# A graph layer and a relational attention layer on one core: the order of work in the last two turns

## The chip, the cores and the metric

The kernel runs on one core of a Trainium2 chip. The metric is the device time of one execution in microseconds; lower is better. Every time below is in microseconds unless it says otherwise.

## The reference

The input is 64 graphs of 256 nodes with 256 features each (`x`), and an adjacency of 256 x 256 for each graph. Two layers follow each other.

```python
# layer 0: two graph-attention steps, residual, norm, feed-forward of width 1024 (relu), residual, norm
h = _gat(_gat(x, adj, W1, a1), adj, W2, a2)
h = _layernorm(x + h, g_ln1, b_ln1)
x = _layernorm(h + relu(h @ w_ff1 + b_ff1) @ w_ff2 + b_ff2, g_ln2, b_ln2)
# layer 1: attention over 8 heads of 32, values by relation (adj == 0, adj == 1), output projection
attn = softmax(q @ k.T / sqrt(32))
out = sum(((attn * (adj == r)) @ (x @ Wv[r] + bv[r])) for r in range(4))
x = _ln(x + out @ Wo + bo, g1, beta1)
# feed-forward of width 1024 (gelu), residual, norm
return _ln(x + gelu(x @ W1 + b1) @ W2 + b2, g2, beta2)
```

All of it is float32. A short check at the end of the kernel adds up some accumulated sums (`low`, `lowg`, `high`, `other`) into one integer `bad`; if it is above zero, a general and slower version of the program runs (with these inputs it does not).

## The kernel before, in words

Two graphs make a unit, so there are 32 units, 0 to 31. A unit has 512 rows (four blocks of 128; blocks 0 and 1 are the first graph, 2 and 3 the second). The work is a pipeline of turns: turn `y_` runs layer 1 of unit `y_`, the feed-forward of layer 0 of unit `x_ = y_ + 1`, and the graph attention of layer 0 of unit `z = y_ + 2` (`turn`, L1275). In turn 30 there is no `z` any more, and in turn 31 only layer 1 of unit 31 is left, together with pieces of the output feed-forward of unit 30 that turn 30 left over (`left`, `piece`). So the last two turns have less independent work to put side by side than those before.

The order is written out by hand for some engines in each turn: in turns with an `X` for PE, SyncE, VectorE and ScalarE, in turn 31 for PE and SyncE alone. There a scheduler orders VectorE and ScalarE by the order in the program and its own estimates; `behind(name)` (L694) holds the instructions issued inside it until after a marked one. What each engine executes is fixed in the built program: each engine takes its instructions in that order.

Products of two 2 x 2 block matrices are done with seven block products instead of eight, named 1 to 7:

- `hidden_seven` (L908) is the first feed-forward product. Its steps are called `2a 1a 2b 1b 5a 5b 3a 3b 6a 6b 7a 7b 4a 4b`; a and b are the halves of the width. Steps 5, 6, 7 and 4 multiply differences of the features' quarters, which VectorE makes by four subtractions (`sub`, L920, tile `tt`). Each step puts two 128 x 256 products into a bank of PSUM. `taken` (L945) moves them to `h1`: a copy on ScalarE (L950) when it is the first for that quarter of `h1`, an add on VectorE (L947) when it is not. Steps 6, 7 and 4 go on accumulating in the bank of step 1, and 5 and 3 in that of step 2, so each of them needs the bank to have been read. `c`, `d` and `s` are activations of finished quarters (L956).
- `HiddenOut` (L997) is the second. `sums` (L1013) are four sums of quarters of `h1`; the products 1, 2, 5, 6, 3, 7, 4 (L1027) are each added to `y` on VectorE (L1035). Products 1, 6, 7 and 4 share a bank, and 5 and 3 another.
- `Projections` (L1046) does the same for queries and keys (`q1` to `q7`) and values (`v1` to `v7`): sums at L1062, products at L1094, copies at L1081, adds at L1078.

A norm is made of moments on VectorE (L865, L866), two or three small operations on Pool (L876 to L879; L879 adds to `high`), an offset `nm` on VectorE (L884) and the application on ScalarE (L894) or Pool (L891); `affine` multiplies by a row (`times`, L903) and adds one (`plus`, L906). The last norm of units 30 and 31 is done in another way: `finish` (L1245) centres and multiplies (L1249), `finished` (L1253) scales and adds (L1256) and stores each block. To turn rows into features, PE transposes blocks (`turned` L512, `to_features` L528, instructions at L518 and L534), and the result is copied out of PSUM (L535).

The check is written after the last turn (L1783 to L1794).

Of the kernel before, what the change touches and what calls it, by code (L numbers as in the profile page):

```python
# [9 lines left out]
F32 = mybir.dt.float32  # L10
I32 = mybir.dt.int32
AF = mybir.ActivationFunctionType
# [373 lines left out]
def narrow_path(  # L386
# [495 lines left out]
    def offsets(blocks, mv, rs, nm):  # L882
        bt = slice(blocks[0], blocks[0] + len(blocks))
        nc.vector.scalar_tensor_tensor(nm[:, bt], mv[:, bt, 0], -1.0, rs[:, bt], op0=ALU.mult, op1=ALU.mult)  # L884

# [21 lines left out]

    def hidden_seven(u, l, hT, w, bi, func, d, tt):  # L908

# [6 lines left out]
        def moving(n):  # L916
            return tt[:, n * N:(n + 1) * N].rearrange("p (t a r) -> p t a r", t=NB, r=32)

        def sub(n, x_, y_):
            nc.vector.tensor_tensor(moving(n), x_, y_, ALU.subtract)  # L920

        sub(0, quarter[0][1], quarter[0][0])
        sub(1, quarter[1][1], moving(0))
        sub(2, quarter[1][1], quarter[0][1])
        sub(3, quarter[1][0], moving(1))
        halves = range(2)
# [64 lines left out]
        def steps(names):  # L991
            for name in names.split():
                step(name)

# [51 lines left out]
    class Projections:  # L1046
# [28 lines left out]
        def taken(s, x, o, b, ps):  # L1075
            y, ps = s.out(x, o, b), ps.rearrange("p (i n) -> p i n", i=2)
            if (x, o, b) in s.begun:
                mark["projected"] = nc.vector.tensor_tensor(y, ps, y, ALU.add)  # L1078
            else:
                s.begun.add((x, o, b))  # L1080
                nc.scalar.copy(y, ps)  # L1081

# [136 lines left out]
    def out_pieces(u, y, h1):  # L1219

        if u == NG - 2:
            s = [io.tile([P, T, N], F32, tag="y", name=f"sq{u}", bufs=4),
                 work.tile([P, T, WX], F32, tag="wh", name=f"wq{u}")[:, :, :N]]
            s += [io.tile([P, T, N], F32, tag=t, name=f"sq{u}_{t}", bufs=1) for t in ("xq", "aq")]
        else:
            s = out_sums(u, 1)
        end = HiddenOut(u, 1, y, h1, w2s, s)
        end.sums(1, 2, 4, 3)
        for p in (1, 2, 5, 6, 3):
            end(p)  # L1230
            if p == 3:
                n = finish(u, y, 0)
            yield
        end(7)
        finished(u, y, 0, *n)
        yield
        end(4)
        finished(u, y, 1, *finish(u, y, 1))
        yield
# [4 lines left out]

    def finish(u, y, b):  # L1245

        n = norm(u, 3, y, range(b * NB, (b + 1) * NB))
        for t in n[0]:
            nc.vector.scalar_tensor_tensor(y[:, t, :], y[:, t, :], n[1][:, t, 0:1], rg4,  # L1249
                                           op0=ALU.subtract, op1=ALU.mult)  # L1250
        return n

# [22 lines left out]
    def turn(y_, x_, z, rest=None):  # L1275
# [49 lines left out]
        with order:  # L1325
# [17 lines left out]
            if X:  # L1343
                X["hT"], moves = normed_features(x_, 0, X["y"], copied=(1, 3, 5, 7, 9, 11), later=True)
            else:
                scores(0, (0,))
            p("v5")
# [71 lines left out]
            else:  # L1419
                powers(0, (1,))  # L1420
                p("q3 v3")
                powers(0, (2, 3))
                p("q6 v6 q7 v7")
# [51 lines left out]
            out_(1)  # L1475
            piece()
            if Z:
# [6 lines left out]
            if Z:  # L1484
                out(1)
                Z["m"].scores(0)
                Z["m"].scores(1)
                Z["m"].exp(0)
                Z["m"].exp(1)
                out.sums(4)  # L1490
                offsets(*n)
                out(2)
                applied_norm(y, *n, range(T))
                Z["m"].masks(0)
                out(5)
                Z["m"].masks(1)
                Z["m"].shares()
            elif X:
                out.product(5)
                out.sums(3)  # L1500
                out.add(5)
            if X and not Z:
                out(6)
            if not Z:
                applied_norm(y, *n)
            else:
                Z["m"].scaled(WH)
# [7 lines left out]
            elif X:  # L1515
                out.sums(4)
                out(7, 3)
            if not Z:
                piece()
                hT = to_features(y, f"h3T{y_}")  # L1520
                hT = [h.rearrange("p (t a r) -> p t a r", t=T, r=32) for h in hT]
                if not X:
                    affine(y, rg3, rb3)
            if waiting and Z:
# [13 lines left out]
            tt = work.tile([P, HPB, NB * N], F32, tag="e", name=f"tt{y_}_1")  # L1538
            second = hidden_seven(y_, 1, hT, w1s, b1, AF.Gelu, Y, tt.rearrange("p a n -> p (a n)"))
            if X:  # L1540
                out.add(4)
                n = moments(x_, 1, X["y"], range(NB, NB + 1), n)
            h1 = Y["h1"] = work.tile([P, FB, TN], F32, tag="h1", name=f"h1{y_}_1", bufs=1)
            if Z:
                second("2a 1a")
# [11 lines left out]
            else:  # L1557
                if X:
                    n = norm(x_, 1, X["y"], mv=n, rest=range(NB + 1, T))
                second("2a 1a 2b 1b")  # L1560
                second("5a 5b")
                if waiting:
                    affine(waiting[0][1], rg4, rb4)
                    stored(*waiting.pop(), slice(0, T))
                if X:
                    offsets(*n)
                    applied_norm(X["y"], *n, [0])
                second("3a")
                if X:
                    applied_norm(X["y"], *n, [1])  # L1570
                second("3b")
                if X:
                    applied_norm(X["y"], *n, [2, 3], True)
                second("6a 6b ca cb da db 7a 7b")
                if X:
                    X["hT"] = with_ones(to_features(X["y"], f"h2T{x_}", (nc.vector.tensor_copy,) * 2))
# [205 lines left out]

    c = work.tile([P, 4], F32, tag="mv", name="checks")  # L1783
    for n, v in enumerate((low, lowg, high, other)):
        nc.vector.tensor_reduce(c[:, n:n + 1], v, AX.X, ALU.add)
    s = work.tile([P, 1], F32, tag="ve", name="checked")
    nc.vector.tensor_reduce(s, c[:, 0:3], AX.X, ALU.add)
    good = work.tile([P, 2], F32, tag="z", name="good")
    nc.vector.tensor_scalar(good[:, 0:1], s, 1e30, None, op0=ALU.is_le)
    nc.vector.tensor_scalar(good[:, 1:2], c[:, 3:4], 0.25 * NG * T * N, None, op0=ALU.is_le)  # L1790
    nc.vector.tensor_tensor(good[:, 0:1], good[:, 0:1], good[:, 1:2], ALU.mult)
    ps = bank("goodp")
    nc.tensor.matmul(ps[:1, :1], good[:, 0:1], ones[:, 0:1], start=True, stop=True)
    nc.vector.tensor_scalar(bad, ps[:1, :1], -1.0, float(P), op0=ALU.mult, op1=ALU.add)  # L1794


@with_exitstack
# [37 lines left out]
```

## Time and profile before

| what | value |
|---|---|
| runs, device time | 2951.56 median of 3 (2950.34 to 2952.9) |
| the profiled execution, device time | 2950.62 |
| its span in the profile | 2949.0 |
| mean granted clock of TensorE | 0.998 of full |
| TensorE busy | 2921.7, 99% of the span |
| VectorE, ScalarE, Pool busy | 2611.3 (89%), 1897.2 (64%), 625.6 (21%) |
| last product of the output feed-forward ends | 2938.2 |
| last finishing step (L1256) of unit 31 ends | 2942.1 |
| `bad` (L1794) is written | 2943.3 |

In the profile PE is TensorE, DVE VectorE, ACT ScalarE, POOL GpSimd and SP SyncE. A line of a timeline gives start, length, engine, line, operation, the tile written and those read, the shapes, a count of merged instructions, and in brackets the idle time of the engine before it with the instruction that ended it. A wait line gives who waited for whom: total, times, longest. A line of a table by stretches gives the stretch, the sum of busy times, and then for PE, weight loads, DVE, ACT and POOL the busy time and the number of instructions, then the granted clock of TensorE as a share of full speed, the DMA engines' share and GB/s. [...]one step of four passes is 0.86 long.

### The profile page before, as it was taken

How to read it: one execution, taken by the hardware profiler on the slowest of the kernel's cores; microseconds unless marked ns; L12 is line 12 of the kernel's file. 1: busy time of each engine (PE TensorE's matmuls, PEld its weight loads, DVE VectorE, ACT ScalarE, POOL GpSimd, SP SyncE). 2: the span in 40 equal slices, each digit the busy share in tenths (PEclk: the TensorE clock that was granted, in tenths of full speed). 3: DMA queues.
4: the chain of work that ended last, by engine and by line, in shares of the span. 5: the costliest groups of instructions: out<-in, count | busy, mean ns of one | idle time of the engine just before them, and what ended most of it. 6: DMA issues, size and time to landing. Idle time of an engine off the chain costs nothing.

```text
span 2949.0 us, 58651 instructions
## 1 busy us (share of the span) xinstructions
PE 2921.7 (99%) x22206; PEld 2505.9 (85%) x22206; DVE 2611.3 (89%) x5028; ACT 1897.2 (64%) x3983; POOL 625.6 (21%) x931
## 2 busy tenths in 40 slices
PE   9999999999999999999999999999999999999997
PEld 7788888888888888888888888888888888888876
DVE  5889899989899889999898998899998989988887
ACT  5566666676676666666766766766667667667652
POOL 3312221122121122221221211222212212112211
PEclk9999999999999999999999999999999999999999
DMA  5011111111111111111111111111111111111000
GB/s 152 13 30 32 39 32 32 24 40 32 37 30 26 34 34 38 33 31 24 40 32 37 31 28 31 36 36 35 29 23 40 32 37 32 28 30 33 18 8 16
DMA packets 408020, 99.27 MB, mean 34 GB/s; under 512 B 357834, under 2 KB 407220, under 8 KB 407732
## 3 DMA queue, kind: packets, MB, share of 16 engines
q1 hardware_dynamic: 406332, 94.13, 14.8%
q8 instruction: 178, 2.92, 0.4%
q0 software_dynamic: 1056, 1.05, 0.1%
q14 instruction: 110, 0.90, 0.1%
q10 hardware_dynamic: 344, 0.28, 0.0%
HBM read 56.78 MB, written 16.78 MB: 25 GB/s over the span
## 4 chain that ended last, share of the span: by engine, by line
PE 97%; DVE 2%; ACT 1%; DMA 0%; issue 0%; POOL 0%; DVEq 0%; POOLq 0%; ACTq 0%
PE yf L1027 27%; PE h1a L938 15%; PE h1b L938 11%; PE po L1143 8%; PE v L1094 6%; PE qk L1094 6%; PE sp L1115 4%; PE hpp L839 4%; PE ygp L850 4%; PE xpp L772 4%; PE yop L850 4%; PE zo L1146 2%; PE rows L781 1%; DMA first<-in_adj_dram 0%; DVE st L865 0%
## 5 line engine op out<-in xcount | busy, mean ns | idle before, releaser
L1124 ACT ACTIVATE e<-sp 128x512 f32<-128x512 f32 x512 | 271.0, 611 | 71.2 <-issue 43.7
L1128 DVE TENSOR_TENSOR ea<-e,aT 128x1024 f32<-128x1024 f32 x256 | 311.1, 1217 | 1.6 <-ACT e L1124 1.6
L894 ACT ACTIVATE y<-y,nm,rs 128x256 f32<-128x256 f32 x442 | 235.1, 592 | 64.0 <-DVE nm L884 63.2
L947 DVE TENSOR_TENSOR h<-h1a,h 128x512 f32<-128x512 f32 x293 | 197.5, 682 | 81.7 <-PE h1a L938 78.5
L950 ACT COPY h<-h1b 128x512 f32<-128x512 f32 x293 | 175.2, 599 | 124.6 <-PE h1b L938 122.8
L956 ACT ACTIVATE h<-h,cols 128x256 f32<-128x256 f32 x512 | 221.9, 502 | 35.7 <-DVE h L947 31.5
L734 POOL COPY hT<-yt 32x256 f32<-32x256 f32 x244 | 211.3, 866 | 144.8 <-DVE yt L717 132.1
L1081 ACT COPY qk<-qk 128x512 f32<-128x512 f32 x128 | 74.3, 580 | 237.4 <-PE qk L1094 236.6
L865 DVE BATCH_NORM_STATS2 st<-y 128x6 f32<-128x256 f32 x512 | 208.7, 409 | 5.7
L876 POOL TENSOR_SCALAR rs<-mv 128x4 f32<-128x4 f32 (+1 forms) x134 | 41.7, 312 | 805.1 <-DVE mv L866 438.5
L1035 DVE TENSOR_TENSOR y<-yf,y 128x256 f32<-128x256 f32 x448 | 185.9, 415 | 29.8 <-PE yf L1027 29.8
L956 ACT ACTIVATE h<-h1a,cols 128x256 f32<-128x256 f32 x256 | 102.6, 465 | 131.9 <-PE h1a L938 131.9
L1156 POOL TENSOR_TENSOR low<-low,rq 128x16 f32<-128x16 f32 x64 | 13.9, 217 | 811.6 <-DVE rq L1155 811.6
L906 DVE TENSOR_TENSOR y<-y,rb 128x1024 f32<-128x1024 f32 x126 | 163.2, 1295 | 2.2
L1133 DVE TENSOR_TENSOR es<-e 128x1024 f32<-128x1024 f32 x128 | 156.0, 1219 | 0.0
L903 DVE TENSOR_TENSOR y<-y,rg 128x1024 f32<-128x1024 f32 x126 | 153.0, 1214 | 0.0
L877 POOL TENSOR_TENSOR rs<-rs,mhalf 128x4 f32<-128x4 f32 (+1 forms) x134 | 139.5, 1041 | 8.3
L1115 PE MATMUL sp<-qk 32*128 32x256 f32 x2048 | 138.4, 394 | 0.0
L938 PE MATMUL h1a<-tt,wf 128*128 128x256 f32 x512 | 137.7, 392 | 0.0
L1143 PE MATMUL po<-e,v 128*32 128x256 f32 x2048 | 135.5, 382 | 0.0
L1143 PE MATMUL po<-ea,v 128*32 128x256 f32 x2048 | 134.5, 379 | 0.0
L717 DVE STREAM_TRANSPOSE yt<-y 128x256 f32<-128x256 f32 x364 | 128.2, 407 | 0.9 <-ACT y L894 0.7
(288 smaller groups left out, 7738.4 us busy)
## 6 DMA issues: line engine op xcount, KB each, us to landing
hT<-yt SPq DMA_DIRECT2D x666, 32.0 KB, 1.8
y<-in_x_dram SPq DMA_DIRECT2D x32, 512.0 KB, 4.1
xq<-in_x_dram SPq DMA_DIRECT2D x240, 64.0 KB, 2.3
aq<-in_adj_dram SPq DMA_DIRECT2D x240, 64.0 KB, 2.3
out_dram<-y SPq DMA_DIRECT2D x30, 512.0 KB
wf<-in_L_gnn_w_ff_dram SPq DMA_DIRECT2D x2, 1024.0 KB, 7.8
w<-in_L_gnn_W_dram SPq DMA_DIRECT2D x2, 1024.0 KB
first<-in_adj_dram POOLq DMA_DIRECT2D x2, 512.0 KB, 9.0
```

What stands on the lines that cost most here:

```text
L734: nc.gpsimd.tensor_copy(to, at)
L850: nc.tensor.matmul(ps[:, i * F:(i + 1) * F], lhs(t, k), rhs(b, k), start=(k == 0), stop=(k == n - 1))
L865: nc.vector.bn_stats(st[:, t, :], y[:, t, :])
L894: mark["normed"] = nc.scalar.activation(y[:, t, :], y[:, t, :], AF.Identity, bias=nm[:, t:t + 1], scale=rs[:, t:t + 1])
L938: nc.tensor.matmul(ps[:, i * N:(i + 1) * N], w_[:, f * P:(f + 1) * P], m, start=first and i == 0, stop=True, skip_group_check=True)
L956: nc.scalar.activation(y, y if ps is None else ps[:, i * N:(i + 1) * N], func, bias=bi[:, f:f + 1])
L1027: nc.tensor.matmul(s.ps[n][:, i * F2:(i + 1) * F2], a[:, k, i * P:(i + 1) * P], w_[:, k, :], start=n in (1, 2, 5) and i == 0 and k == 0, s ...
L1094: nc.tensor.matmul(ps[:, i * N:(i + 1) * N], l, r, start=n in (1, 2, 5) and i == 0, stop=True, skip_group_check=True)
L1115: nc.tensor.matmul(ps[a][:, j * N:(j + 1) * N], k_[hp, m, j0:j0 + P], q[hp, m, b * N:(b + 1) * N], start=True, stop=True)
L1124: nc.scalar.activation(e[:, a, :], ps[a], AF.Exp, scale=isd)
L1128: nc.vector.tensor_tensor(ea[:, a:a + 2, :], e[:, a:a + 2, :], ab[:, None, :].to_broadcast([P, 2, NB * N]), ALU.mult)
L1143: nc.tensor.matmul(po[hp, m * N:(m + 1) * N], vs[:, hp], w[:, a, j * N:(j + 1) * N], start=(n == 0), stop=(n == len(terms) - 1))
```

## The change

In the last two turns:

- Unit 31's layer-0 feed-forward, in turn 30: sum 4 and product 3 come before sum 3 and product 7.
- Unit 30's hidden layer, in turn 30: the order is now `times` of unit 29's last affine, then steps 3a and 3b, then the offset and the application of unit 31's norm, steps 6a to 7b, and only then `plus` of that affine and the store of unit 29.
- Turn 31, projections: no exponential of the first scores is issued before the copy of v5; the first two stand behind it (mark `placed`, `fifths`), the other two behind the copy of v3. Sums of unit 30's `h1` (1, 2, 4, 3) stand behind the first add of the values (`projected31_v`).
- Turn 31, features of the normed unit: by graph. The transposes of blocks 0 and 1 come before product 4 of unit 30, and steps 2a and 1a of the hidden layer before the transposes of blocks 2 and 3; the copies are of 128 x 256, three on ScalarE and one on VectorE. The four differences are made after that (step name `t`). Before, all eight transposes, two copies of 128 x 512 and the differences came ahead of step 2a.
- Unit 30's `centred` and `finished` of the first graph stand behind unit 31's second offset (`offset`), and the affine of unit 31 behind an add of the hidden layer (`added`).
- Unit 31: `centred` of the first graph comes after product 7's add.
- The check is made in two parts: `low`, `lowg` and `other` are reduced in turn 31 (in the built program beside the second graph's division), `high` after the last centring, and the two comparisons go as both operands into one product of 1 x 1.

The order of the built programs differs nowhere before unit 31's sum 3, which ran at 2835.8 in the profile before; up to there only line numbers differ. The diff, cut to its core:

```diff
-    def hidden_seven(u, l, hT, w, bi, func, d, tt):
+    def hidden_seven(u, l, hT, w, bi, func, d, tt, begin=True):
...
+        if begin:
+            differences()
...
+                if name == "t":
+                    differences()
...
             if (x, o, b) in s.begun:
                 mark["projected"] = nc.vector.tensor_tensor(y, ps, y, ALU.add)
+                mark.setdefault(f"projected{s.u}_{x}", mark["projected"])
             else:
                 s.begun.add((x, o, b))
-                nc.scalar.copy(y, ps)
+                mark["placed"] = nc.scalar.copy(y, ps)
...
-        end.sums(1, 2, 4, 3)
+        if u == NG - 2:
+            with behind(f"projected{NG - 1}_v"):
+                end.sums(1, 2, 4, 3)
+        else:
+            end.sums(1, 2, 4, 3)
         for p in (1, 2, 5, 6, 3):
             end(p)
             if p == 3:
-                n = finish(u, y, 0)
+                n = norm(u, 3, y, range(NB))
             yield
         end(7)
-        finished(u, y, 0, *n)
-        yield
+        if u == NG - 2:
+            yield
+        with behind("out" if u == NG - 1 else "offset"):
+            centred(y, *n)
+            finished(u, y, 0, *n)
+        if u == NG - 1:
+            verdict = checks()
+            yield
         end(4)
-        finished(u, y, 1, *finish(u, y, 1))
+        n = norm(u, 3, y, range(NB, T))
+        centred(y, *n)
+        if u == NG - 1:
+            verdict()
+        finished(u, y, 1, *n)
         yield
...
+    def checks():
+
+        c = work.tile([P, KB * N // 32], F32, tag="rq", name="checks")
+        good = work.tile([P, 2], F32, tag="z", name="good")
+        for n, v in enumerate((low, lowg, other)):
+            nc.vector.tensor_reduce(c[:, n:n + 1], v, AX.X, ALU.add)
+        nc.vector.tensor_add(c[:, 0:1], c[:, 0:1], c[:, 1:2])
+        nc.vector.tensor_scalar(good[:, 1:2], c[:, 2:3], 0.25 * NG * T * N, None, op0=ALU.is_le)
+
+        def verdict():
+            nc.vector.tensor_reduce(c[:, 3:4], high, AX.X, ALU.add)
+            nc.vector.tensor_scalar(good[:, 0:1], c[:, 3:4], c[:, 0:1], 1e30, op0=ALU.add, op1=ALU.is_le)
+            ps = bank("goodp")
+            nc.tensor.matmul(ps[:1, :1], good[:, 0:1], good[:, 1:2], start=True, stop=True)
+            nc.vector.tensor_scalar(bad, ps[:1, :1], -1.0, float(P), op0=ALU.mult, op1=ALU.add)
...
             else:
-                scores(0, (0,))
+                scores(0, ())
             p("v5")
...
-                powers(0, (1,))
+                mark["fifths"] = mark["placed"]
+                with behind("fifths"):
+                    powers(0, (0, 1))
                 p("q3 v3")
-                powers(0, (2, 3))
+                with behind("fifths"):
+                    powers(0, (2, 3))
...
             elif X:
                 out.product(5)
-                out.sums(3)
+                out.sums(4)
                 out.add(5)
...
+            if not X:
+                piece()
+                h3T = work.tile([P, KB, TN], F32, tag="hT", name=f"h3T{y_}")
+                ph = turned(y, f"h3T{y_}", range(NB))
+
+                def half(b_):
+                    ns = slice(b_ * N, (b_ + 1) * N)
+                    nc.scalar.copy(h3T[:, 1, ns], ph[1][:, ns])
+                    (nc.scalar.copy, nc.vector.tensor_copy)[b_](h3T[:, 0, ns], ph[0][:, ns])
+
+                half(0)
...
             elif X:
-                out.sums(4)
-                out(7, 3)
+                out.sums(3)
+                out(3, 7)
...
+            if not X:
+                piece()
             h1 = Y["h1"] = work.tile([P, FB, TN], F32, tag="h1", name=f"h1{y_}_1", bufs=1)
+            if not X:
+                second("2a 1a")
+                turned(y, f"h3T{y_}", range(NB, T), ph)
+                half(1)
+                second("t")
...
-                second("2a 1a 2b 1b")
+                second("2a 1a 2b 1b" if X else "2b 1b")
+                if not X:
+                    with behind("added"):
+                        affine(y, rg3, rb3)
                 second("5a 5b")
                 if waiting:
-                    affine(waiting[0][1], rg4, rb4)
-                    stored(*waiting.pop(), slice(0, T))
+                    times(waiting[0][1], rg4)
+                second("3a 3b")
                 if X:
                     offsets(*n)
                     applied_norm(X["y"], *n, [0])
-                second("3a")
-                if X:
                     applied_norm(X["y"], *n, [1])
-                second("3b")
-                if X:
                     applied_norm(X["y"], *n, [2, 3], True)
                 second("6a 6b ca cb da db 7a 7b")
+                if waiting:
+                    plus(waiting[0][1], rb4)
+                    stored(*waiting.pop(), slice(0, T))
```

More of the change, by code (lines that the diff above doesn't have):

```diff
@@ L883, in offsets @@
         bt = slice(blocks[0], blocks[0] + len(blocks))
-        nc.vector.scalar_tensor_tensor(nm[:, bt], mv[:, bt, 0], -1.0, rs[:, bt], op0=ALU.mult, op1=ALU.mult)
+        mark["offset"] = nc.vector.scalar_tensor_tensor(nm[:, bt], mv[:, bt, 0], -1.0, rs[:, bt], op0=ALU.mult, op1=ALU.mult)
     def applied_norm(y, blocks, mv, rs, nm, part=None, gpsimd=False):
@@ L920, in sub, with differences @@
             nc.vector.tensor_tensor(moving(n), x_, y_, ALU.subtract)
[L922 to L925, printed above, removed]
+        def differences():
+            sub(0, quarter[0][1], quarter[0][0])
+            sub(1, quarter[1][1], moving(0))
+            sub(2, quarter[1][1], quarter[0][1])
+            sub(3, quarter[1][0], moving(1))
+        if begin:
+            differences()
         halves = range(2)
@@ L992, in steps @@
             for name in names.split():
-                step(name)
+                if name == "t":
+                    differences()
+                else:
+                    step(name)
         return steps
@@ L1227, in out_pieces @@
         end = HiddenOut(u, 1, y, h1, w2s, s)
-        end.sums(1, 2, 4, 3)
+        if u == NG - 2:
+            with behind(f"projected{NG - 1}_v"):
+                end.sums(1, 2, 4, 3)
+        else:
+            end.sums(1, 2, 4, 3)
         for p in (1, 2, 5, 6, 3):
@@ L1243, in stored, with centred @@
         nc.sync.dma_start(out[b].rearrange("b (c p) f -> p (b c) f", p=P), y[:, bt, :])
[L1245 to L1249, printed above, removed]
+    def centred(y, blocks, mv, rs, nm):
+        for t in blocks:
+            nc.vector.scalar_tensor_tensor(y[:, t, :], y[:, t, :], mv[:, t, 0:1], rg4,
                                            op0=ALU.subtract, op1=ALU.mult)
-        return n
+    def checks():
[11 more added lines that the diff above has]
+            nc.vector.tensor_scalar(bad, ps[:1, :1], -1.0, float(P), op0=ALU.mult, op1=ALU.add)
+        return verdict
     def finished(u, y, b, blocks, mv, rs, nm):
@@ L1475, in turn @@
             out_(1)
-            piece()
+            if X:
+                piece()
             if Z:
@@ L1503, in turn @@
                 out(6)
+            if not X:
[7 more added lines that the diff above has]
+                half(0)
+                hT = [h3T[:, k].rearrange("p (t a r) -> p t a r", t=T, r=32) for k in range(KB)]
             if not Z:
@@ L1515, in turn @@
             elif X:
-                out.sums(4)
-                out(7, 3)
-            if not Z:
+                out.sums(3)
+                out(3, 7)
+            if X and not Z:
                 piece()
@@ L1521, in turn @@
                 hT = [h.rearrange("p (t a r) -> p t a r", t=T, r=32) for h in hT]
-                if not X:
-                    affine(y, rg3, rb3)
             if waiting and Z:
@@ L1538, in turn @@
             tt = work.tile([P, HPB, NB * N], F32, tag="e", name=f"tt{y_}_1")
-            second = hidden_seven(y_, 1, hT, w1s, b1, AF.Gelu, Y, tt.rearrange("p a n -> p (a n)"))
+            second = hidden_seven(y_, 1, hT, w1s, b1, AF.Gelu, Y, tt.rearrange("p a n -> p (a n)"), bool(X))
             if X:
@@ L1542, in turn @@
                 n = moments(x_, 1, X["y"], range(NB, NB + 1), n)
+            if not X:
+                piece()
             h1 = Y["h1"] = work.tile([P, FB, TN], F32, tag="h1", name=f"h1{y_}_1", bufs=1)
+            if not X:
[3 more added lines that the diff above has]
+                second("t")
             if Z:
@@ L1780, in narrow_path @@
             turn(u, u + 1, u + 2, second_half)
[L1783 to L1794, printed above, removed]
 @with_exitstack
```

## The prediction, made before the changed kernel was run

> **What bounds the kernel now.** I read the busy shares and the chain of waits first, then TensorE's waits, then the timeline and the stretches of the last 120 us.
>
> ```profile
> PE 2921.7 (99%) x22206; PEld 2505.9 (85%) x22206; DVE 2611.3 (89%) x5028; ACT 1897.2 (64%) x3983; POOL 625.6 (21%) x931
> PE 97%; DVE 2%; ACT 1%; DMA 0%; issue 0%; POOL 0%; DVEq 0%; POOLq 0%; ACTq 0%
> ```
>
> TensorE (PE) works without a break, so the change can only win where PE stands still. TensorE's waits from 2700 us on:
>
> ```profile
> PE goodp L1793 <- DVE good L1791: 4.7, 1, 4.7
> PE yf L1027 <- DVE y L1035: 2.8, 3, 1.5
> PE h1a L938 <- DVE h L947: 2.1, 2, 2.0
> PE qk L1094 <- DVE qk L1078: 0.9, 1, 0.9
> PE h1b L938 <- DVE h3T L535: 0.8, 1, 0.8
> PE h3T31p L534 <- ACT y L894: 0.8, 2, 0.6
> ```
>
> All lie in the last two turns (units 30 and 31), which is also where the built programs differ: the first changed instruction runs at about 2835.7. The timeline gives the places (start, length, in brackets the idle before):
>
> ```profile
> 2838.00 3.84 PE L1027 MATMUL yf<-wf,eaq 128*128 128x128 f32 x32 [0.52 <-DVE y L1035]
> 2855.18 3.05 PE L938 MATMUL h1a<-tt,w 128*128 128x256 f32 x8 [1.97 <-DVE h L947]
> 2865.92 1.13 PE L1094 MATMUL qk<-tq,wqks 128*128 128x256 f32 x4 [0.95 <-DVE qk L1078]
> 2906.06 2.05 PE L1027 MATMUL yf<-w2t,h 128*128 128x128 f32 x16 [1.48 <-DVE y L1035]
> 2915.03 1.97 PE L938 MATMUL h1b<-tt,w1s 128*128 128x256 f32 x8 [0.32 <-DVE tt L920]
> 2936.17 2.05 PE L1027 MATMUL yf<-w2t,h 128*128 128x128 f32 x16 [0.85 <-DVE y L1035]
> ```
>
> A wait costs more than its idle time: the modelled end of a pass lies 0.16 after the next could have started, and the first pass after a wait takes 0.10 more. So 1.97 is worth 2.23. The stretches (the columns end in PEclk, DMA share, GB/s) show a second cost:
>
> ```profile
> 2852.69:2856.10 3.41, 1.44 (x7) 0.80 (x5) 1.99 (x4) 2.75 (x5) 1.09 (x2) 1.00 0.43 154
> 2856.10:2859.51 3.41, 3.41 (x12) 2.89 (x12) 1.78 (x3) 3.40 (x9) 0.00 (x0) 0.50 0.00 0
> 2903.89:2907.30 3.41, 1.93 (x18) 1.74 (x17) 2.84 (x9) 0.42 (x1) 1.10 (x3) 1.00 0.22 77
> ```
>
> After 3.41 us with PE busy for 1.44, the clock was half for 3.41 us; after 1.93 it stayed full. The steps from 2855.18 to the first projection at 2861.35 took 6.18; at the full pace of this trace (8 and 8 passes of 0.216, 8 transposes of 0.109, 0.10 once) they take 4.43. The half clock cost 1.75.
>
> [...]`nm` (L884) started at 2853.14 behind the affine (L903, L906), though Pool had finished its input at 2851.15. [...]a product into a bank waits for the add that reads it (the 0.52 at 2838.00).
>
> **The parts, one by one.** Durations are of the trace; VectorE (DVE) slots are from start to start: 0.34 for a 128x256 add, 0.61 for 128x512, 1.14 for 128x1024, 0.39 for a centring or finishing step. Times are on the clock of the profile before.
>
> A. *Unit 31's sums 4 and 3 and products 3 and 7 change places.* Product 3 goes to another bank than 6 and waits for no add; product 7 follows 1.79 later, when sum 3 (ends 2839.16) is just done. The 0.52 goes: 0.52+0.16+0.10 = 0.78, less a wait of some 0.1 at product 3 (its bank's add ends 2837.29, PE is free at 2837.32). Gain **0.65**.
>
> B. *Unit 30's hidden layer.* Before, product 7a waited for the add of 6a, that for the copy of 3a on ScalarE, that stood behind a normalization that needs `nm`, and `nm` behind 2.28 of unit 29's affine. Now the copies precede the norms, and only the times (1.14) precedes `nm`; the add of 6a runs at 2851.73 to 2852.42, PE is free at 2852.40. What is late next: 0.07+0.10 there. Gain 2.23-0.17 = **2.06**, and the half clock (**1.75**) has no cause. But the plus (1.22) now stands ahead of the two copies of unit 31's features: they run 2856.24 to 2857.54, and the first projection waits 0.07+0.10. Loss **0.17**.
>
> C. *Unit 31's projections.* Sum 1 (1.14) moves behind the add that the q5 product waits for, but that queue starts later relative to PE: copies to 2857.54, times, four differences, plus, the add ends 2861.76. PE is free at 2860.54, so q5 waits 1.27 (0.95 before, 1.11 from pass to pass). Loss **0.16**. The copy of v5 goes ahead of the table load and two exponentials, which removes 0.55 at v3 (0.82 in all); in exchange q3's copy comes after table load 1.28 and two exponentials (at 2867.96 to 2868.55), and the add of q6, needed by q7, comes after it: q7 waits 0.96+0.10, against 0.15 before. Sum **0**. From here to the attention's end nothing else changes.
> A to C: 0.65+2.06+1.75-0.17-0.16 = 4.13.
>
> D. *Unit 31's features by graph.* VectorE's queue: the checks add 0.3 at 2898.4; unit 30's two centrings and finishing steps (1.7 with their wait) go behind unit 31's moments, which end at 2905.2 instead of 2906.9. The add of product 7 ends 2905.63 (2906.01), product 4 starts 0.39 earlier with four of eight transposes already done, and 2a starts at 2907.57 instead of 2910.99. 2a, 1a, four transposes, 2b, 1b keep PE until 2911.46. Then 5a needs the first difference. Ahead of it on VectorE: `nm` (Pool's 1.2 after the moments, 2906.43), 2 centrings, 2 finishing steps, add of product 4, moments (to 2909.5), 2 centrings inside Pool's 1.5 (pow ends 2910.98), 2 finishing steps 0.8, add of 1a 0.61, the copy 0.34, add of 1b 0.61, the difference 0.42: it ends 2913.77. So 5a starts at 2913.82 instead of 2915.03, after a wait of **2.36**. The copy (128x256 from PSUM) isn't in the trace: at least the 0.34 of an add of that size, at most the 0.61 of the 128x512 copy; I take 0.34. The next six steps take 5.35 (5.66 before). Then third sum 1.14 stands ahead of the add of 7b, waiting for two activations, so 4b waits 0.79+0.10. Output product 1: 2923.80 instead of 2924.44. Gain **0.64**; 1.2 more were 7b's add in front, 0.3 less with the dear copy.
>
> E. *Add of product 7 ahead of unit 31's centrings.* Product 7 ends 2935.32, its add 2935.76, product 4 at 2935.81 instead of 2936.17. Gain **0.36**.
>
> F. *The check.* After the last finishing step (ends 2942.09) came ten small steps up to `bad` (2943.31): 1.22. Three reductions and both comparisons lie earlier now; `high` is reduced in Pool's pow wait, the comparison between the two finishing steps, the product beside the second. `bad` ends 0.11 after the second: gain 1.11, less 0.02 of order. Gain **1.09**. The 5.7 from `bad` to the end (loading it, branches, instruction fetches) stay; the last stores land within 1.7 of issue and are covered by these 5.7; SyncE loads `bad` 0.35 later behind the last store, but it waits 2.5 there for others anyway.
>
> Sum: 4.13+0.64+0.36+1.09 = **6.2**. The profiled execution took 2950.62 (span 2949.0, 1.6 around it), so 2944.4 of its kind. The median of the runs is 0.94 above it, and I keep that: 2951.56-6.2 = **2945.3**.
>
> **Rivals.**
> 1. *The sum as it stands.* 2945.3, chance 0.43.
> 2. *A new half clock.* The wait of 2.36 in D is longer than the 1.97 that had one. [...]six steps run at half clock, 1.7 more: 2947.0. For it: the two stretches above[...]. Chance 0.28.
> 3. *The median before had no half clock.* Then 1.75 isn't there to win: 2947.1, and 2948.8 together with 2. [...]Against: the profiled execution, which had it, lies at the low end of the runs. Chance 0.14.
> 4. *VectorE's queue is shorter than my sum,* 5a waits about 1.3 and 4b not at all: 2943.5. Chance 0.1.
> 5. *Slower.* Strict order turned against PE: unit 30's last finishing steps wait for Pool with the adds, the copy and the differences of unit 31 behind them. From a wait at 5a of some 5.5 (3.1 more than summed) two half-clock windows fit behind it (3.4): 2945.3+6.5 = 2951.8. Pool's three operations would need 4.6 instead of 1.5; its first took 1.03 at most here. Chance 0.05.
>
> **Numbers.** About 0.2% (5.9 us) is what a measurement of this kernel can tell from no change; the bound is 2945.66. Cases 1 and 4 lie below it, but case 1 by 0.4 alone, so I leave a sixth of it above and give a few of case 2 below: faster 0.50, within 0.46, slower 0.04. The range reaches from case 4 with the cheap ends to cases 2 and 3 together: 2942.8 to 2949.0.
>
> **What would show it.** Right: no wait over 0.2 at 7a of unit 30 and PEclk 1.00 there; q5 waiting about 1.3, q7 about 1.0; 5a of unit 31 waiting 2 to 2.5 on VectorE, 4b 0.8; `bad` 0.1 after the last finishing step. Wrong: 5a without a wait (case 4), PEclk 0.5 behind it (case 2), or a span that moves by less than 3 although these waits are as said.

## The result and the profile after

| | before | after |
|---|---|---|
| median of 13 runs each | 2952.14 | 2945.32 (2943.12 to 2947.24) |
| ratio of the times, 95% interval | | 0.9975 (0.9968 to 0.9982) |
| the profiled execution, device time | 2950.62 | 2946.93 |
| its span | 2949.0 | 2945.3 |

The change makes the kernel 0.25% faster by this table. Some executions (3 of the 13 before and none of the 13 after; later 8 of 49 of the kernel before, 8 of 14 of the kernel "B alone", 8 of 22 of "late", a few of most others) took some 8 us more at a lower mean clock (of the kernel before 0.994 to 0.996 against 0.997 to 0.999), and no profile fell on one, so every median from here on is of the other executions (2951.67 of 10 before, 6.35 or 0.22% above the 2945.32 after).

Kernels are compared below by their traces, counted from one instruction ahead of the change, the last pass of unit 30's attention output product (L850, at 2833.53 before and 2834.25 after). A pass is one instruction of TensorE in the profile; a step of the hidden layer, two products of 128 x 256, stands there as four passes (0.86 from start to start), so such a product is two passes here.

The busy shares and the chain look as before:

```profile
PE 2921.1 (99%) x22206; PEld 2502.4 (85%) x22206; DVE 2609.6 (89%) x5027; ACT 1898.9 (64%) x3985; POOL 624.9 (21%) x931
PE 97%; DVE 1%; ACT 1%; DMA 0%; issue 0%; POOL 0%; POOLq 0%; DVEq 0%; ACTq 0%
```

So the difference is in TensorE's waits. Those of the kernel after from 2826 us on (who for whom: total, times, longest):

```profile
PE goodp L1286 <- DVE good L1284: 3.7, 1, 3.7
PE h1b L942 <- DVE tt L920: 2.4, 1, 2.4
PE qk L1102 <- DVE qk L1085: 1.8, 2, 1.1
PE yf L1034 <- DVE y L1042: 0.7, 2, 0.5
PE h1a L942 <- DVE h L951: 0.6, 1, 0.6
```

And their places, in the timeline of the same kernel:

```profile
2853.35 1.99 PE L942 MATMUL h1a<-tt,w 128*128 128x256 f32 x8
2862.67 1.13 PE L1102 MATMUL qk<-tq,wqks 128*128 128x256 f32 x4 [1.09 <-DVE qk L1085]
2870.21 1.13 PE L1102 MATMUL qk<-tq,wqk 128*128 128x256 f32 x4 [0.74 <-DVE qk L1085]
2901.98 2.05 PE L1034 MATMUL yf<-w2t,h 128*128 128x128 f32 x16 [0.20 <-DVE y L1042]
2910.32 3.35 PE L942 MATMUL h1b<-tt,w1s 128*128 128x256 f32 x8 [2.39 <-DVE tt L920]
2921.08 1.13 PE L942 MATMUL h1a<-tt,w 128*128 128x256 f32 x4 [0.62 <-DVE h L951]
2933.44 2.05 PE L1034 MATMUL yf<-w2t,h 128*128 128x128 f32 x16 [0.52 <-DVE y L1042]
```

Step 7a of unit 30 (first line) stands without a bracket: its 1.97 is gone. Product 4 of unit 30 waits 0.20 instead of 1.48, that of unit 31 0.52 instead of 0.85, and the 0.52 at unit 31's layer-0 product, the 0.55 at v3 and the 0.78 at the first product of unit 31's hidden layer are gone too. New are the waits at q7, at 5a (2.39 instead of 0.32) and at 4b. Behind 5a the first eight passes take 3.35 instead of 1.97. The stretches show why (columns as in the front):

```profile
2907.33:2910.74 3.41, 1.02 (x5) 0.62 (x4) 3.31 (x8) 3.02 (x5) 0.07 (x1) 1.00 0.22 77
2910.74:2914.16 3.41, 3.41 (x10) 2.70 (x9) 2.71 (x4) 1.45 (x3) 0.00 (x0) 0.50 0.00 0
```

The new wait fell into one stretch of 3.41, TensorE was busy for 1.02 of it, and then ran at half clock (0.50) for 3.41. From 5a to output product 1 of unit 31 this execution took 11.73; one without the half clock (below) took 10.14. So the half clock that the change takes away behind 7a of unit 30 came back in turn 31, at a price of 1.6.

### The profile page after: what moved, and what is told of

Read it like the earlier page. It is cut to its first block, busy times and chain, and to the rows that moved or that the text cites. A ratio compares the mean times of both kernels' runs of the same rounds, so it can differ in the third digit from the quotient of the medians.

```text
span 2945.3 us, 58649 instructions
## 1 busy us (share of the span) xinstructions
PE 2921.1 (99%) x22206; PEld 2502.4 (85%) x22206; DVE 2609.6 (89%) x5027; ACT 1898.9 (64%) x3985; POOL 624.9 (21%) x931
## 3 DMA queue, kind: packets, MB, share of 16 engines
q0 software_dynamic: 1056, 1.05, 0.1%
## 4 chain that ended last, share of the span: by engine, by line
PE 97%; DVE 1%; ACT 1%; DMA 0%; issue 0%; POOL 0%; POOLq 0%; DVEq 0%; ACTq 0%
PE yf L1034 27%; PE h1a L942 15%; PE h1b L942 12%; PE po L1151 8%; PE v L1102 6%; PE qk L1102 6%; PE sp L1123 4%; PE hpp L839 4%; PE ygp L850 4%; PE xpp L772 4%; PE yop L850 4%; PE zo L1154 2%; PE rows L781 1%; DMA first<-in_adj_dram 0%; ACT h L960 0%
```

## Experiments

All times in the table are counted from the common instruction, in each profiled execution. "5a" and "product 1" are those of unit 31. "`bad` loaded" is the end of VectorE's load of `bad`, 0.58 behind its write in every kernel.

| kernel | q1 of unit 31 | attention output of unit 31 (L850) | 5a | product 1 | `bad` loaded |
|---|---|---|---|---|---|
| before | 27.82 | 63.76 | 81.50 | 90.90 | 110.36 |
| after | 23.61 | 59.80 | 76.07 | 87.80 | 105.95 |
| B alone | 24.18 | 60.37 | 79.31 | 88.64 | 108.10 |
| B undone | 27.21 | 62.20 | 78.48 | 88.62 | 106.78 |
| C undone | 23.61 | 59.79 | 76.07 | 87.80 | 105.96 |
| F undone | 23.61 | 59.81 | 76.09 | 86.23 | 105.35 |
| D undone, first | 23.61 | 59.81 | 81.73 | 91.99 | 110.15 |
| D undone, second | 23.61 | 59.81 | 77.07 | 86.40 | 104.56 |
| filled | 23.61 | 59.81 | 77.09 | 87.13 | 105.29 |
| late | 23.61 | 59.81 | 73.51 | 83.99 | 103.06 |
| late, sums late | 23.61 | 59.81 | 73.52 | 83.10 | 102.08 |
| late, split | 23.61 | 59.81 | 73.51 | 83.11 | 101.26 |
| late, split, q5 | 23.53 | 59.35 | 73.06 | 82.65 | 100.81 |

Columns agree to 0.02 wherever the orders of the engines are the same and no half clock lies between: the trace resolves a tenth of a microsecond, where the medians of the kernel before in four series of runs lie between 2950.36 and 2951.67.

**B alone** (kernel before with unit 30's new order) **and B undone.**

```diff
                 if waiting:
-                    affine(waiting[0][1], rg4, rb4)
-                    stored(*waiting.pop(), slice(0, T))
-                if X:
-                    offsets(*n)
-                    applied_norm(X["y"], *n, [0])
-                second("3a")
+                    times(waiting[0][1], rg4)
+                second("3a 3b")
+                if X:
+                    offsets(*n)
+                    applied_norm(X["y"], *n, [0])
...
                 second("6a 6b ca cb da db 7a 7b")
+                if waiting:
+                    plus(waiting[0][1], rb4)
+                    stored(*waiting.pop(), slice(0, T))
```

> The kernel before with step B alone: unit 30's hidden layer takes the new order (times, 3a and 3b, offset and application, 6a to 7b, then plus), all else as before. My theory: step 7a no longer waits 1.97 for an add (2.06 gained with the pass to pass terms), and with that wait the half clock of 3.41 behind it goes (1.75): about 3.6 us less than before where the half clock was there, and PEclk 1.00 from 7a to the first projection. Theory of case 3 (the half clock is not in most executions of the kernel before): 1.9 less. A third theory, that the wait only moves to the next adds and copies: less than 1 us.

> The changed kernel with step B taken back. My theory: the wait of about 2 at 7a of unit 30 is back, so 1.9 us more than the changed kernel, and 3.6 more where the half clock follows it; the stretches behind 7a then show PEclk near 0.50[...]. If B is worth little, as the theory says that puts the gain in the features by graph, the time stays within 1 us of the changed kernel.

B alone: q1 comes at 24.18 instead of 27.82, so 3.64 earlier, as summed; the wait at 7a and the half clock behind it are gone. The end is only 2.26 earlier in this execution, since another half clock fell on the first products of unit 31's hidden layer (2906.93 to 2910.34). The median, 2947.43 (6 runs), is 3.70 below the 2951.13 (41 runs) of the kernel before measured beside it. B undone: the wait is back, and the half clock with it. Its timeline and stretches:

```profile
2856.88 3.04 PE L942 MATMUL h1a<-tt,w 128*128 128x256 f32 x8 [1.97 <-DVE h L951]
```

```profile
2854.30:2857.71 3.41, 1.44 (x7) 0.87 (x5) 1.99 (x4) 2.66 (x5) 1.10 (x2) 1.00 0.43 154
2857.71:2861.12 3.41, 3.41 (x13) 2.79 (x12) 1.78 (x4) 3.40 (x8) 0.00 (x0) 0.50 0.00 0
```

q1 is 3.60 later than in the changed kernel, but the attention's output only 2.40, and so is the end (106.78 against 104.38, worked out below for a changed kernel at full clock). The 1.2 between is the wait at q5: TensorE comes later, VectorE and ScalarE do not, so there is nothing to wait for. My 3.6 for the end was wrong: in the finished kernel B is worth 2.4, since its last 1.2 is handed to the next wait. The median was 2948.14 (11 runs).

**C undone.**

```diff
-                scores(0, ())
+                scores(0, (0,))
...
-                mark["fifths"] = mark["placed"]
-                with behind("fifths"):
-                    powers(0, (0, 1))
+                powers(0, (1,))
                 p("q3 v3")
-                with behind("fifths"):
-                    powers(0, (2, 3))
+                powers(0, (2, 3))
...
-        if u == NG - 2:
-            with behind(f"projected{NG - 1}_v"):
-                end.sums(1, 2, 4, 3)
-        else:
-            end.sums(1, 2, 4, 3)
+        end.sums(1, 2, 4, 3)
```

> The changed kernel with step C taken back (first scores' exponentials as before, sums of unit 30 not held behind the first add of the values). The built orders of VectorE and TensorE are the same as in the changed kernel; on ScalarE the copies of v5 and of q3 and v3 change places with exponentials. My theory: 0.55 of waiting comes back at v3 (0.8 with the pass to pass terms) and 0.7 goes at q7: the same time within 0.3 us. Rival: the order of the copies is a part of the gain, then v3 waits and q7 waits too, and it costs 0.8 or more.

The waits of this kernel at the projections:

```profile
2862.34 1.13 PE L1102 MATMUL qk<-tq,wqks 128*128 128x256 f32 x4 [1.09 <-DVE qk L1085]
2867.02 1.13 PE L1102 MATMUL v<-wvs,h2T 128*128 128x256 f32 x4 [0.55 <-ACT v L1089]
```

The 0.55 is back at v3, the 0.74 at q7 gone, and 59.79 stands against 59.80: ScalarE's new order is worth nothing. The median was 2945.47 (10 runs).

**F undone**: the check is written after the last turn again.

```diff
-        if u == NG - 1:
-            verdict = checks()
...
-        if u == NG - 1:
-            verdict()
...
+    c = work.tile([P, 4], F32, tag="mv", name="checks")
+    for n, v in enumerate((low, lowg, high, other)):
+        nc.vector.tensor_reduce(c[:, n:n + 1], v, AX.X, ALU.add)
```

> The changed kernel with the check written at the end again, as before. My theory: ten small VectorE steps come between the last finishing step and bad, and the time from the last finishing step to bad is 1.2 instead of 0.15: 1.0 us more than the changed kernel. Rival: the end is set by the last stores or by SyncE, and bad's lead is lost there: no difference.

From the end of product 4 to the load of `bad` this kernel took 5.67, the changed one 4.71: 0.96. (Its profile had no half clock before the last product, so its row up to product 1 shows the changed kernel at full clock; its product 4 ends at 99.67, and with the 4.71 the load of `bad` would end at 104.38.) The median was 2946.25 (19 runs). The end of VectorE's queue, with F undone and in the kernel after:

```profile
2934.52 0.88 DVE L1291 SCALAR_TENSOR_TENSOR y<-y,rs,rb 128x256 f32<-128x256 f32 x2 [0.75 <-POOL rs L877]
...
2936.48 0.14 DVE L1852 TENSOR_SCALAR bad<-goodp 1x1 int32<-1x1 f32 x1 [0.37 <-PE goodp L1851]
```

```profile
2938.48 0.49 DVE L1294 SCALAR_TENSOR_TENSOR y<-y,rs,rb 128x256 f32<-128x256 f32 x1 [0.50 <-POOL rs L877]
2938.89 0.21 DVE L1284 TENSOR_SCALAR good<-checks 128x1 f32<-128x1 f32 x1
2939.01 0.48 DVE L1294 SCALAR_TENSOR_TENSOR y<-y,rs,rb 128x256 f32<-128x256 f32 x1
2939.47 0.15 DVE L1287 TENSOR_SCALAR bad<-goodp 1x1 int32<-1x1 f32 x1
```

This kernel also bears on the half clock. In the profile before and in the one after, the half-clock stretches start whole multiples of 3.413 apart (before: 2856.10 is 831 of them behind 19.62; after: 2910.74 is 847 behind 19.65). Here the wait at 5a is the same (2.41), but stretches counted so, from the half-clock stretch at this kernel's end, are cut elsewhere:

```profile
2906.31:2909.72 3.41, 1.78 (x8) 1.44 (x9) 3.41 (x8) 2.33 (x6) 0.00 (x0) 1.00 0.22 77
2909.72:2913.13 3.41, 3.41 (x17) 2.87 (x16) 1.78 (x3) 2.00 (x4) 0.00 (x0) 1.00 0.00 0
```

Only 1.63 of the wait lies in the first of them; the rest lies in the one before. Behind the 1.78 busy the clock stayed full (1.00). Of the four profiles that have a wait of 2.4 at 5a, two have a half clock behind it (after, C undone) and two do not (F undone, B undone). Up to 5a the order of TensorE and VectorE is the same in F undone and in the kernel after, the wait too, and they are 1.6 apart: what is seen to differ is the place of the stretches (the one in which the wait ends starts 1.63 ahead of 5a in F undone, the one in the kernel after 2.99 ahead).

**Filled**: 16 idle products inside the wait at 5a.

```diff
+                    for _ in range(16):
+                        nc.tensor.matmul(ph[1][:, :P], ident, ident, start=True, stop=True)
                 second("5a 5b")
```

> The changed kernel with 16 idle products of 128x128 (ident by ident, into a bank whose contents are already copied out) on TensorE while it waits for the first difference ahead of step 5a of unit 31; they add about 2.05 of work inside the wait of 2.4 and nothing else. My theory: step 5a starts where it did, but [...]no half clock follows in any execution: from 5a to the first output product 10.15 (as in the run without half clock) and not 11.7, and 1.6 times the share of disturbed executions less in the mean. Rival (the slower steps are due to VectorE's and ScalarE's queues behind 5a, and the clock is a mere sign): 11.7 stays. Second rival (idle products hinder the copies or the difference): 5a starts later.

I had counted passes as products: 16 products of 128x128 are 32 passes in the timeline and took 3.6 instead of 2.05, and 5a started 1.0 later, behind them and not behind VectorE. From 5a on it went at full clock (10.04 to product 1), as two of the four profiles with the wait did too. So the second rival's sign came from my own size, and the run is no test of what filling the wait would save; median 2945.91 (12 runs). What there is instead are the two pairs of stretches above: half clock behind 1.02 busy, full behind 1.78.

**D undone**, twice: eight transposes, two copies of 128x512 and the differences ahead of 2a; in the program unit 30's finishing steps stand where they were before.

```diff
-                ph = turned(y, f"h3T{y_}", range(NB))
...
-                half(0)
...
-            if X and not Z:
+            if not Z:
                 piece()
                 hT = to_features(y, f"h3T{y_}")
...
-                second("2a 1a")
-                turned(y, f"h3T{y_}", range(NB, T), ph)
-                half(1)
-                second("t")
```

> The changed kernel with step D taken back: all eight transposes, two copies of 128x512 and the differences ahead of step 2a, and unit 30's last centrings and finishing steps where they were before. My theory (step D is worth 0.64 to 0.9 where the clock stays full, and the wait that it makes at 5a of unit 31 draws a half clock of 1.6 in some executions): step 5a waits 0.3 to 0.5 instead of 2.4 but starts later; measured from the last attention product ahead of the change, the check's end is 0.9 later than in a changed kernel without that half clock (104.4 for the span from there to bad, so 105.3) and 0.7 earlier than in one with it (105.95). Rival (step D was worth its 1.2 at step 5a, whatever the clock): 1.2 or more later than 105.95.

The load of `bad` ended at 110.15, 4.2 later than in the kernel after: inside the rival's open range, but not for its reason. The scheduler of turn 31 had put the copy of the features behind the last finishing steps, which wait 0.75 for Pool: the first product waited 2.45, and two half-clock stretches followed (median 2951.18, 11 runs). So it did not undo D alone. The second one holds those steps behind the copy (a mark on the copy):

```diff
+            yield
+            with behind("features"):
+                centred(y, *n)
+                finished(u, y, 1, *n)
```

> Step D taken back once more, this time with VectorE's order as in the kernel before: unit 30's last two centrings and finishing steps are held behind the copy of unit 31's features (in the first undoing the scheduler had put them ahead of it). My theory (step D by itself is worth the 0.64 of the prediction, as long as no half clock comes): the copy runs at once, the first product waits 0.8 for it as in the kernel before, and counted from the last layer-1 output product ahead of the change the check ends 0.6 to 0.9 later than the changed kernel at full clock (104.4, so 105.0 to 105.3). Rival (step D is worth more, 2.4, as the first undoing less its two half-clock stretches has it): 106.8.

The first product waits 0.78 for the copy as before, 5a comes at 77.07, product 1 at 86.40, the load of `bad` ends at 104.56 (median 2946.75, 16 runs). Against the changed kernel at full clock (86.23, 104.38) that is 0.17 or 0.18, less than the 0.6 to 0.9 I expected: what this undoing takes back, the features by graph above all, gains 0.98 up to 5a and loses 0.81 behind it. But the scheduler again did not restore VectorE's order: over the stretch from the attention's output to product 1 this kernel is itself 0.55 faster than the kernel before. That does not come from product 4 of unit 30: that starts 0.39 earlier than before, but the transposes then wait longer for ScalarE (1.01 instead of 0.61), and the first product comes 13.70 behind unit 31's attention output in both. The wait at 5a is gone (0.32 before). VectorE, in the kernel before and here:

```profile
2910.24 0.69 DVE L535 COPY h3T<-h3T31p 128x512 f32<-128x512 f32 x1 [0.78 <-PE h3T31p L534]
2910.85 0.17 DVE L866 BATCH_NORM_AGGREGATE mv<-st 128x2 f32<-128x6 f32 x1
2912.54 0.88 DVE L1256 SCALAR_TENSOR_TENSOR y<-y,rs,rb 128x256 f32<-128x256 f32 x2 [0.75 <-POOL rs L877]
```

```profile
2905.85 0.30 DVE L866 BATCH_NORM_AGGREGATE mv<-st 128x2 f32<-128x6 f32 x2
2906.79 0.69 DVE L1228 COPY h3T<-h3T31p 128x512 f32<-128x512 f32 x1 [0.64 <-PE h3T31p L534]
2908.19 0.88 DVE L1308 SCALAR_TENSOR_TENSOR y<-y,rs,rb 128x256 f32<-128x256 f32 x2
```

Before, the last moments of unit 30 stand behind the copy, so the finishing steps wait 0.75 for Pool, and the first difference, behind them, is late for 5a (2914.89; 0.75 less would be ahead of TensorE's end of 1b at 2914.71). Here the moments stand ahead of the copy, Pool is done in time, and the difference ends at 2910.53, ahead of 5a at 2911.10. In the kernel after a wait of 0.74 for Pool does stand ahead of the difference (below), so this 0.55 is not a part of D: the run measures D against a better order than that of the kernel before.

**Late, sums late, split, q5**: four kernels that go on from the change. VectorE's queue ahead of 5a, in the kernel after, shows what to move:

```profile
2902.91 0.87 DVE L1270 SCALAR_TENSOR_TENSOR y<-y,mv,rg 128x256 f32<-128x256 f32 x2
2903.70 0.87 DVE L1294 SCALAR_TENSOR_TENSOR y<-y,rs,rb 128x256 f32<-128x256 f32 x2
...
2905.83 0.86 DVE L1270 SCALAR_TENSOR_TENSOR y<-y,mv,rg 128x256 f32<-128x256 f32 x2
2907.43 0.88 DVE L1294 SCALAR_TENSOR_TENSOR y<-y,rs,rb 128x256 f32<-128x256 f32 x2 [0.74 <-POOL rs L877]
2908.23 0.68 DVE L951 TENSOR_TENSOR h<-h1a,h 128x512 f32<-128x512 f32 x1
2908.83 0.41 DVE L1554 COPY h3T<-h3T31p 128x256 f32<-128x256 f32 x1
```

Eight steps for unit 30, which nobody waits for, and Pool's 0.74 stand ahead of the copy that 5a needs.

```diff
+        if u == NG - 2:
+            end(4)
+            n_ = norm(u, 3, y, range(NB, T))
+            yield
+            with behind("out"):
+                centred(y, *n)
+                finished(u, y, 0, *n)
+                centred(y, *n_)
+                finished(u, y, 1, *n_)
+            yield
+            return
...
+                    next(pieces)
+                    piece()
                     for _ in pieces:
                         pass
```

> The changed kernel with unit 30's eight last centring and finishing steps held behind unit 31's first output product instead of ahead of its features' copy and differences. My theory (the wait of 2.4 at 5a is VectorE's queue: 3.2 of these steps and 0.74 of waiting for Pool stand in it): 5a does not wait or waits under 0.4, so 2.2 to 2.7 less at 5a; the wait of 4b for the add behind the third sum (0.6 to 0.8) stays; no cause for the half clock: 2 to 2.5 us less than the changed kernel without half clock, 3.6 to 4.1 less than with it. Rival (other queues are as late: ScalarE's table load and activations with the copies of 2b and 5a behind them): steps 3a, 6b or 7a wait in place of 5a, and less than 1 us is gained.

The second of the four has this besides:

```diff
         else:
-            end.sums(1, 2, 4, 3)
+            with behind("added"):
+                end.sums(1, 2, 4, 3)
```

> The kernel of the run before in this call (unit 30's last steps late) with unit 31's sums of the hidden layer's quarters held behind the last add of the hidden layer, too. My theory: step 4b's wait of 0.6 to 0.8 goes, so 0.7 to 0.9 less than in that run, and the sums, 1.14 each, are still made before product 5 needs the first of them. Rival: product 5 or 6 of the output layer waits for the later sums, and the gain is given back: no difference or 0.5 more.

Late: 5a comes at 73.51 (2.58 earlier, wait 0.16), product 1 2.24 earlier, and the end 1.3 earlier than the changed kernel at full clock, not the 2 to 2.5 I expected: 0.9 went to a new wait of 0.64 at unit 31's product 3, for the add of product 5 that stood behind the eight steps. Its median was 2943.95 (14 runs). With the sums behind the hidden layer's last add, 4b's wait of 0.62 goes and the end comes 0.98 earlier: 2942.27 (6 runs). Then the eight steps in two groups of four, the second behind product 6's add, and in the last kernel the plus of unit 29 moved:

```diff
                 finished(u, y, 0, *n)
+            yield
+            with behind("out"):
                 centred(y, *n_)
...
                     next(pieces)
                     piece()
+                    for _ in range(3):
+                        next(pieces)
+                    piece()
```

```diff
-                    plus(waiting[0][1], rb4)
-                    stored(*waiting.pop(), slice(0, T))
...
+                with behind(f"projected{NG - 1}_v"):
+                    plus(kept[0][1], rb4)
+                stored(*kept.pop(), slice(0, T))
```

> The kernel with unit 30's last steps late and the sums late, but the eight steps in two groups: four behind unit 31's first output product as before, four behind product 6's add, where VectorE stood idle for 1.8. My theory (in the kernel with all eight in one group, product 3 waited 0.55 for the add of product 5 that stood behind them): that wait goes, 0.7 to 0.8 less from the same start (102.08 to 101.3), and no new wait at product 7. Rival: the add of product 3 is now behind the second group and product 7's add with it, so product 4 waits longer: no gain.

> The kernel of the run before in this call, with unit 29's last plus (1.22 on VectorE) and its store moved further behind, from ahead of the first add of unit 31's projections to behind the first add of its values. My theory: in the changed kernel step q5 waits 1.09 for that add, but ScalarE's copy of q1, which the add needs, ends at 2861.90, just when VectorE comes free at 2861.93, so the wait stays: less than 0.1 gained. Rival (the wait is VectorE's queue alone, as my prediction counted it): the wait of 1.09 goes, 1 us less.

TensorE's waits in the split kernel, from 2826 on:

```profile
PE goodp L1300 <- DVE good L1298: 3.7, 1, 3.7
PE qk L1102 <- DVE qk L1085: 1.8, 2, 1.1
PE yf L1034 <- DVE y L1042: 0.7, 2, 0.5
PE h1b L942 <- ACT h L954: 0.2, 1, 0.2
```

The end comes 0.82 earlier, as summed; median 2942.17 (5 runs). For q5 neither theory held: 0.45 was gained. I had taken the end of the copy of v1 (27.67 from the common start) for that of q1 (27.19); the add needs q1 alone. With the plus moved, VectorE is free early, the add starts at 27.21 when ScalarE's copy ends, and q5 waits 0.81: ScalarE, busy with 16 activations, is the next bound. This last kernel has a median of 2941.68 (5 runs, 2939.44 to 2943.44), 0.9963 of the kernel before (0.9949 to 0.9977). By the traces it ends 3.57 earlier than the changed kernel at full clock; the intervals of the two ratios still overlap.

## Why the prediction was right, step by step

| step | predicted | measured | from |
|---|---|---|---|
| A | 0.65 | 0.57 | start of the next transposes (unit 30's features), 8.14 and 7.57 |
| B, with the half clock | 3.64 | 3.64 | B alone, q1 |
| C | -0.16 | -0.25 | rest of 3.96 at the attention's output |
| D, full clock | 0.64 | 0.72 | 27.14 and 26.42 (F undone) from there to product 1 |
| E | 0.36 | 0.33 | product 1 to the end of product 4, 13.78 and 13.45 |
| F | 1.09 | 0.96 | end of product 4 to the load of `bad`, 5.67 and 4.71 |
| sum, full clock in turn 31 | 6.22 | 5.98 | |
| with the half clock behind 5a | 4.5 | 4.41 | the profiled execution |

The mechanisms were the predicted ones but for parts of C, D and F. B: the order of work on VectorE and ScalarE (before, `nm` started at 2853.14 behind the affine, 1.99 after Pool had finished its input), and a half clock with the wait (0.50 from 2856.10 to 2859.51). The predicted waits were counted from pass to pass, 0.16 more than idle time: q5's 1.27 is 1.11 of idle time and was 1.09, q7's 0.96 is 0.80 and was 0.74, 4b's 0.79 is 0.63 and was 0.62, and 5a's 2.36 is 2.20 and was 2.39. The copy of 128x256 took a slot of 0.33, the cheap end.

C's -0.25 is not C's: from q1 to the attention's output it is 35.94 before, and 36.19 in B alone as in the kernel after. Of it 0.14 is the longer wait at q5, the term predicted, and 0.10 is q1's longer first pass, which the prediction had under B. (Its own figures for v3 and q7, 0.82 won and 0.91 lost, leave -0.09, where it wrote 0; and Pool's first operation, under rival 5, took up to 1.05, not 1.03.)

D's sum is right in part by luck: 5a came 1.47 earlier (17.74 and 16.27 from the attention's output), not 1.21, and from there to product 1 it took 10.14, not 9.98. I gave the gain to the features by graph together with unit 30's later finishing steps; neither undoing restored the order of the kernel before (against the second one's better order D is worth 0.17), so how the 0.72 divides stays open.

F is 0.13 smaller because of the comparison between the two finishing steps, which the prediction put at 0.02: the second step starts 0.53 behind the first (2938.48 and 2939.01), where the pair with F undone follows at 0.40. From the end of the last step to the write of `bad` the gain is the predicted 1.09 (1.22 before, 0.13 after).

Rival 1, the sum as it stands, is what an execution at full clock would do, as pieced together with F undone; no profile of the kernel after is one. Rival 2, the new half clock, is what the profiled execution and one other did, two of four. The prediction gave it 0.28. Two of four is too few to tell 0.28 from a half. Rival 3 is not supported as a rule: both profiles with the wait at 7a have its half clock. It may hold for a few executions: with no half clock at the start (in F undone the common instruction then runs 1.7 earlier, below) the kernel before would take 2948.9 by my estimate (2950.62 less 1.7), and 2947.46 was seen. Rivals 4 and 5 did not happen. So the traces account for 5.98 in an execution at full clock and 4.41 in one with the half clock, about 5.2 if each is half of them. The medians differ by 6.35, and by 5.8, 6.0 and 5.0 if the kernel before is taken from three later series (2951.13 of 41 runs, 2951.35 of 35, 2950.36 of 20). They scatter around the traced gain, and the profiled executions already differ by up to 3.95 where the change begins (below), so medians of a dozen runs cannot say more. The forecast of 2945.3 came so near 2945.32 with some luck, since its sum leaves out the half clock that half of the profiles with this wait have.

## What to carry to other kernels

When one engine is nearly always busy, list its few waits, and for each what stands ahead of the releasing instruction in its queue; work that nobody waits for (here the finishing steps of a unit that is done) goes behind what the busy engine needs, and in small groups, so that it does not become the next wait. A wait on TensorE can cost twice: here both profiles with the 1.97 at 7a also have a half clock behind it (1.75 in the profile before), and of the four with 2.4 at 5a two have one (1.6) and two have none. So count both costs for a wait that a change takes away, and both for one that it makes. An undoing counts only if the order on every engine is what it was: compare the built orders before reading its time. Neither undoing of D passed that.

## What the runs showed of the hardware that was not expected

Up to the last product, the half clock came behind stretches in which TensorE had worked. The half-clock stretches in the last two turns were 3.41 or 3.42 long, and where the 3.41 ahead of one had the full clock, TensorE was busy in it for 1.02 to 1.85 (1.02 after, 1.10 D undone, 1.44 before and B undone, 1.85 B alone); after 1.78 (F undone) and 1.93 (before) it stayed full. The busy time of the profile decides nothing between: in one execution of B undone the clock was half after 1.44 from 2854.30 (shown with that run) and full after 1.45 in the first stretch here; after the second, of B alone, it was half.

```profile
2912.32:2915.73 3.41, 1.45 (x7) 1.33 (x8) 3.41 (x7) 2.33 (x5) 0.00 (x0) 1.00 0.22 77
2903.52:2906.93 3.41, 1.85 (x11) 1.16 (x10) 2.57 (x9) 1.68 (x3) 0.37 (x2) 1.00 0.00 0
```

What sets these stretches apart was not shown.

A part of the spread between the profiled executions comes from the first 25 us; the other runs were not traced. F undone has the full clock from 9.4 to 23.06, and its common instruction runs at 2831.9. Before and after have one half-clock stretch there (19.62 to 23.03 and 19.65 to 23.06), and theirs runs at 2833.5 and 2834.3. B undone and late have two (14.40 to 17.82 and 21.23 to 24.65; 14.96 to 18.38 and 21.79 to 25.20), and theirs runs at 2835.8 and 2835.7. That is 1.5 to 2.4 from each to the next. The second one of B undone came after a stretch with TensorE busy for 3.13:

```profile
17.82:21.23 3.41, 3.13 (x22) 2.58 (x21) 0.42 (x3) 0.75 (x2) 0.00 (x0) 1.00 1.07 388
21.23:24.65 3.42, 3.42 (x14) 2.93 (x14) 0.00 (x0) 0.57 (x2) 0.00 (x0) 0.50 0.94 299
```

The one of the kernel after came behind 3.13 busy too (16.24 to 19.65, 23 passes, 15 of them one column wide), while F undone stayed full behind 3.28 in the same stretch. Why was not shown.
